# Six DMAs of the first pair begun by GpSimd, and three experts' w2 extended ahead of the first attention pair

## The chip, the cores and the metric

The kernel runs on one core of one Trainium2 chip. The metric is the device time of one execution in microseconds (us), as the median of several. An engine works through its own instructions in the order in which they stand in the program: TensorE (PE in the profile), VectorE (DVE), ScalarE (ACT), GpSimd (POOL), and SyncE (SP), which here only begins DMAs. An engine waits on semaphores for what other engines and DMAs have to deliver, and while it waits, everything behind the waiting instruction on that engine waits too.

## The reference

The kernel computes an attention layer and a mixture-of-experts layer, both with residuals, on an input of 2 x 2048 x 256 floats.

```python
def attention(x):              # 2 x 2048 x 256, one head of width 128
    q, k, v = x @ wq.T, x @ wk.T, x @ wv.T
    q, k = rope(q), rope(k)
    w = softmax(q @ k.T / sqrt(128))
    return (w @ v) @ wo.T

def ffn(z):                    # two loops, 8 experts, the 2 best for each token
    for _ in range(2):
        n = rmsnorm(z, norm_w)
        cw = normalised top-2 of softmax(n @ router_w)
        z = z + sum_e cw[e] * ((silu(n @ w1[e]) * (n @ w3[e])) @ w2[e])
    return z

x = x + layernorm(attention(layernorm(x)))
x = x + layernorm(ffn(layernorm(x)))
```

The expert matrices w1 and w3 are 256 x 512 and w2 is 512 x 256, all in float32. The router's product of the second loop is taken from the expert's output directly: beside w2[e] the kernel keeps w2[e] times the scaled router matrix (512 x 8), so that one matrix product gives a row of the output and its share of the next router logits. Computing these 8 extra columns is what "extending" w2 means.

## The kernel before, in words

The program first projects the input to q, k and v in eight blocks of 512 rows (until about 86 us), then runs attention, then the expert jobs. The change lies in attention.

Attention is written as one loop over `step` (L1593). A query tile has 128 rows; there are 16 for each of the 2 batches, and two tiles make a pair, so pairs 0 to 7 belong to the first batch and 8 to 15 to the second. The scores of a tile are computed in four chunks of 512 keys. Each step works at several stages of the pipeline at once, in this order of the program:

- `move_chunks` (L1465): for the first batch alone, the exponents of a pair are moved by DMA from tile `pr` to a standing area (`wall` in the profile, since it lies in the weights of experts 4 to 7, which are loaded only after pair 7). A chunk takes four DMAs of 128 KB, a pair 16. They begin five steps after the score, at the second tile of a pair.
- `exponents` (L1443): ScalarE, four steps after the score, because the smallest of all four chunks (`nm`) is needed first.
- `turn_chunks` (L1473): VectorE transposes an eighth of the moved pair into `pt`. The first one of a pair (a = 0) needs all 16 moves of that pair.
- `score` (L1424): two matmul instructions, then a reduction on VectorE and after the fourth chunk the one that gives `nm`.
- `values` (L1497), by the table `WHEN` (L1584): the products with v, for pair p at its steps a = 3 to 7 and at a = 0 of the next.
- `leave` (L1510): a generator that is moved on once in every step and brings a finished pair through the output projection and two normalisations; its GpSimd work belongs to it.
- the extension of w2 and the scaling of w1 and w3 (`scale_expert`, L238, GpSimd).

With `p, a = divmod(step - 15, 8)`, pair 0 begins its transposes at step 15, and each pair has the steps a = 0 to 7. Steps 0 to 14 hold the scores of the first tiles and nothing for a pair to turn yet. In pair 6 the scores of six steps are missing, because those of the second batch begin six steps later (`LATER`).

`extend(e)` (L1394) is a generator of six pieces: the load of w2[e] into `wb` (four DMAs of 128 KB begun by SyncE), four transposes on VectorE (`wT`, L1403), and last 16 matmul instructions (`tp_e`, L1411) with a copy by VectorE into place (L1418). In the kernel before, its pieces for expert e stand at the end of the step: the load at a = 5 of pair e - 1, one transpose at each of a = 0 to 3 of pair e, the matmuls and the copy at a = 4. So every pair of the first batch carries one expert, and `wb` has one buffer.

The order on each engine is the order of the program; nothing is rearranged. SyncE begins, in each pair, the moves of the next pair, the load of one w2 and the load of the input rows `xr`.

Of the kernel before, what the change touches and what calls it, by code (L numbers as in the profile page):

```python
# [10 lines left out]
F32 = mybir.dt.float32  # L11
# [8 lines left out]
P = 128  # L20
# [9 lines left out]
def attn_moe_kernel(  # L30
# [16 lines left out]
    nc = tc.nc  # L47

    ctx.enter_context(tc.manual_schedule())
    B, S, D = x.shape  # L50
    HD = wq.shape[0]
    E, _, F = w1.shape
    ND = D // P
    NF = F // P
# [1132 lines left out]
    with tc.tile_pool(name="proj1", bufs=1, **left) as p1, tc.tile_pool(  # L1187
        name="proj", bufs=2, **left
# [190 lines left out]
    with tc.tile_pool(name="prob", bufs=6, **left) as pprob, tc.tile_pool(  # L1379
# [14 lines left out]

        def extend(e):

            wb = pw.tile([P, NF, D], F32, tag="wb", name="wb")
            load_blocks(wb.rearrange("p a d -> p (a d)"), w2[e], 0, NF)
            yield

            wT = pw.tile([P, ND, NF, 4, 32], F32, tag="wT", name="wT")
            for k in range(NF):
                nc.vector.transpose(  # L1403
                    out=wT[:, :, :, k, :].rearrange("p c a t -> p a c t"),
                    in_=wb[:, k, :].rearrange("p (a d c) -> p a c d", a=4, c=ND),
                )
                yield
            ps = ps_t.tile([P, NF, E], F32, tag="tp", name="tp_e")
            for f in range(NF):
                for c in range(ND):  # L1410
                    nc.tensor.matmul(  # L1411
                        ps[:, f, :],
                        lhsT=wT[:, c, f].rearrange("p k t -> p (k t)"),
                        rhs=wr[:, c, :],
                        start=(c == 0),
                        stop=(c == ND - 1),
                    )
            nc.vector.tensor_copy(extended(e) if e < HELD else ext[:, e - HELD], ps)  # L1418
            yield
# [45 lines left out]
        def move_chunks(p, c):  # L1465

            pr = prs.pop((p, c))
            for a in range(4):
                nc.sync.dma_start(
                    out=standing(p)[32 * c : 32 * (c + 1), :, a], in_=pr[32 * a : 32 * (a + 1)]  # L1470
                )

# [116 lines left out]
        first = turns[0][0].before(ps_t, "tp", keep=False)  # L1589
        credit = 0  # L1590
        ahead = iter(range(-GATHER, 0))
        chunks = {u if u // (NT * NKC) in EXCHANGED else u + LATER: u for u in range(NS * NP)}
        for step in range(NS * NP + LEAD + LATER + 1):  # L1593
            u = chunks.get(step - NKC - 1)
            if u is not None and u // (NT * NKC) in EXCHANGED:
                t, c = divmod(u, NKC)
                p, i = divmod(t, QG)
                if i == QG - 1:
                    move_chunks(p, c)
            u = chunks.get(step - NKC)  # L1600
            if u is not None:
                exponents(u)
            p, a = divmod(step - LEAD - LATER, NS)
            if 0 <= p < NP:
                (turn_chunks if p // (NP // B) in EXCHANGED else transposes)(p, a)
            for gen in list(leaving):
                if next(gen, True):
                    leaving.remove(gen)
            if (p, a) >= (ROUTED + 1, 1):
                credit = min(credit, 0) + STEP  # L1610
                while credit > 0:
                    took = next(first, None)
                    if took is None:
                        break
                    credit -= took
                if credit > 0:
                    for m in itertools.islice(ahead, 1):
                        fetch_rows(m)
            u = chunks.get(step)
            if u is not None:  # L1620
                score(u)
            if a == 0 and 0 < p <= NP:
                values(p - 1, NS - 1)
                leaving.append(leave(p - 1))
                next(leaving[-1])
                if p == NP // B:

                    bigs[0].close()
                    rpool = ctx.enter_context(tc.tile_pool(name="route", bufs=1, **right))
                    spool = ctx.enter_context(tc.tile_pool(name="rows", bufs=2, **right))  # L1630
            if 0 <= p < NP:
                for g in WHEN.get(a, ()):
                    values(p, g)
            if a == NS // 2 and HELD <= p - NP // B + HELD < E:
                load_expert(p - NP // B + HELD)
                nc.gpsimd.tensor_copy(
                    extended(p - NP // B + HELD), ext[:, p - NP // B, :, :]
                )
            if a == NS - 3 and -1 <= p < E - 1:
                extending = extend(p + 1)  # L1640
                next(extending)
            elif 0 <= p < E and a < NS - 3:
                next(extending)
            e = p if p < NP // B else p - 1 - NP // B + HELD
            if (0 <= p < HELD or p > NP // B) and e < E:
                if a == 2:
                    scaling = scale_expert(e)
                    next(scaling)
                elif a == 5:
                    next(scaling)  # L1650
# [126 lines left out]
```

## Time and profile before

| | |
|---|---|
| median of 3 runs | 1215.41 us (1214.83 to 1219.23) |
| profiled execution, its own time | 1218.09 us |
| its span (first to last instruction) | 1216.3 us |
| mean granted TensorE clock | 0.985 |
| TensorE busy | 1148.5 us, 94% |
| VectorE, ScalarE, GpSimd busy | 654.4, 426.8, 626.8 us |
| first score | 86.25 us |
| first transpose of pair 0 | 109.03 us |
| first transpose of pair 7 | 235.15 us |
| output of pair 7 leaves PSUM (`oT`) | 257.75 us |

How to read the lines: a line of the timeline has the start in us, the duration, the engine, the line of the program, the operation, the tile written and those read, and the number of instructions; in brackets stands how long the engine was idle before, and what ended the idle time. SPq lines are the times in which SyncE hands over a DMA, not those in which the data moves. In a table of windows the last three columns are the granted TensorE clock (1.00 is full), the mean busy share of the 16 DMA engines, and what they moved in GB/s.

### The profile page before, as it was taken

How to read it: one execution, taken by the hardware profiler on the slowest of the kernel's cores; microseconds unless marked ns; L12 is line 12 of the kernel's file. 1: busy time of each engine (PE TensorE's matmuls, PEld its weight loads, DVE VectorE, ACT ScalarE, POOL GpSimd, SP SyncE). 2: the span in 40 equal slices, each digit the busy share in tenths (PEclk: the TensorE clock that was granted, in tenths of full speed). 3: DMA queues.
4: the chain of work that ended last, by engine and by line, in shares of the span. 5: the costliest groups of instructions: out<-in, count | busy, mean ns of one | idle time of the engine just before them, and what ended most of it. 6: DMA issues, size and time to landing. Idle time of an engine off the chain costs nothing.

```text
span 1216.3 us, 16506 instructions
## 1 busy us (share of the span) xinstructions
PE 1148.5 (94%) x4098; PEld 708.7 (58%) x4098; DVE 654.4 (54%) x1703; ACT 426.8 (35%) x971; POOL 626.8 (52%) x1011
## 2 busy tenths in 40 slices
PE   6987999899989799999999999999999999999995
PEld 4543666566756445555555566556666555565664
DVE  4645888767797377533333558324683333368314
ACT  4444334235544422222222552224522222245224
POOL 3560585455522444455444684455844554478753
PEclk9998999999999999999999999999999999999997
DMA  4715797725301578788877977498664897897825
GB/s 145 212 42 133 167 201 191 166 87 147 105 26 36 145 205 233 197 212 237 230 201 207 278 195 198 147 240 272 218 191 146 233 256 219 227 265 231 257 89 181
DMA packets 229417, 224.15 MB, mean 184 GB/s; under 512 B 83088, under 2 KB 177168, under 8 KB 229328
## 3 DMA queue, kind: packets, MB, share of 16 engines
q1 hardware_dynamic: 205840, 158.98, 48.2%
q0 software_dynamic: 20752, 60.97, 17.5%
q10 hardware_dynamic: 2736, 3.16, 0.8%
q8 instruction: 39, 0.64, 0.2%
q14 instruction: 50, 0.41, 0.1%
HBM read 122.77 MB, written 83.47 MB: 170 GB/s over the span
## 4 chain that ended last, share of the span: by engine, by line
PE 62%; DMA 2%; DVE 1%; issue 1%; ACT 1%; POOL 0%; SPq 0%; ACTq 0%; DVEq 0%; POOLq 0%
PE p L1028 39%; PE py L1087 20%; PE tp_x L1014 1%; PE sum L917 1%; DMA xg<-zd,token 1%; DMA given<-given 0%; DMA zd<-y 0%; PE ps_l L665 0%; DMA xs<-xg 0%; DVE ln_st L198 0%; DMA given<-y,to 0%; SPq L998 0%; DVE z L794 0%; DVE ln_mv L199 0%; ACT z L786 0%
## 5 line engine op out<-in xcount | busy, mean ns | idle before, releaser
L1028 PE MATMUL p<-wall,xT 128*128 x1136 | 513.0, 595 | 5.9 <-ACT a L1037 4.3
L1028 PEld LDWEIGHTS p<-wall,xT 128*128 128x128 f32 x1136 | 211.9, 191 | 218.2 <-issue 207.0
L1101 POOL DMA_INDIRECT given<-y,to x142 | 144.0, 1014 | 303.8 <-ACT y L1100 209.1
L1087 PE MATMUL py<-wall,gT 128*128 x1136 | 272.0, 383 | 2.6 <-ACT y L1100 2.0
L1087 PEld LDWEIGHTS py<-wall,gT 128*128 128x128 f32 x1136 | 215.4, 190 | 94.2 <-issue 64.1
L1053 DVE TENSOR_TENSOR g<-a,p 128x512 f32<-128x512 f32 x138 | 94.5, 684 | 263.2 <-issue 214.3
L1100 ACT ACTIVATE y<-py,rms 128x264 f32<-128x264 f32 (+1 forms) x142 | 67.8, 477 | 315.3 <-PE py L1087 290.0
L969 POOL DMA_INDIRECT xg<-zd,token x142 | 142.0, 1000 | 29.8 <-issue 24.8
L1037 ACT ACTIVATE a<-p,rms 128x512 f32<-128x512 f32 x142 | 97.6, 687 | 151.0 <-PE p L1028 89.4
L1430 PE MATMUL sc<-qkT 128*128 128x512 f32 x256 | 134.9, 621 | 12.0 <-ACT pr L1450 11.2
L1502 PE MATMUL po<-pt,v 128*128 128x256 f32 x512 | 129.3, 386 | 3.5 <-DVE pt L1476 3.1
L1502 PEld LDWEIGHTS po<-pt,v 128*128 128x128 f32 x512 | 98.3, 194 | 56.8 <-issue 35.9
L263 DVE STREAM_TRANSPOSE gT<-gb 128x512 f32<-128x512 f32 x138 | 97.4, 706 | 53.0 <-DMA gb<-gd 46.6
L1450 ACT ACTIVATE pr<-sc,nm 128x512 f32<-128x512 f32 x128 | 87.9, 692 | 97.3 <-DVE nm L1440 64.1
L1437 DVE TENSOR_REDUCE m<-sc 128x1 f32<-128x512 f32 x128 | 87.8, 687 | 36.4 <-PE sc L1430 36.1
L185 POOL TENSOR_TENSOR rds<-rs_v,neg_half 128x2 f32<-128x2 f32 (+1 forms) x24 | 19.8, 823 | 94.3 <-DVE rs_v L184 93.7
L1430 PEld LDWEIGHTS sc<-qkT 128*128 128x128 f32 x256 | 45.0, 196 | 31.0 <-ACT pr L1450 22.0
L1476 DVE STREAM_TRANSPOSE pt<-wall 128x512 f32<-128x512 f32 x64 | 43.8, 686 | 11.4 <-DMA wall<-pr 10.8
L243 POOL TENSOR_SCALAR wall<-wall,nwp 128x1024 f32<-128x1024 f32 x16 | 45.9, 2867 | 0.2
L1273 PE MATMUL pm<-wqkvT,hT 128*128 128x392 f32 x128 | 45.8, 501 | 0.0
L263 DVE STREAM_TRANSPOSE xT<-xb 128x256 f32<-128x256 f32 x88 | 35.8, 408 | 17.6 <-DMA xb<-xs 16.6
L1489 PE MATMUL tp_p<-ident,pr 128*128 128x128 f32 x256 | 40.2, 276 | 5.0 <-ACT pr L1450 3.6
(274 smaller groups left out, 1147.8 us busy)
## 6 DMA issues: line engine op xcount, KB each, us to landing
gd<-g SPq DMA_DIRECT2D x138, 256.0 KB
gb<-gd SPq DMA_DIRECT2D x276, 128.0 KB
wall<-pr SPq DMA_DIRECT2D x128, 128.0 KB
xs<-xg SPq DMA_DIRECT2D x44, 257.0 KB
xb<-xs SPq DMA_DIRECT2D x176, 64.0 KB
given<-given SPq DMA_DIRECT2D x16, 528.0 KB
wall<-in_L_ffn_w SPq DMA_DIRECT2D x16, 512.0 KB
z<-zd POOLq DMA_DIRECT2D x32, 256.0 KB
```

Of the source, the lines that this page charges most:

```text
L263: nc.vector.transpose(out=dst.rearrange("p c (a t) -> p a c t", t=32), in_=src.rearrange(f"p (a {columns}) -> p a c d", a=4, c=dst.shape[1]),)
L969: i = nc.gpsimd.indirect_dma_start(out=self.xg[:, k, :], out_offset=None, in_=zd[self.loop][: (SPLIT if self.i < WHOLE else T) * P, :], in ...
L1028: nc.tensor.matmul(ps, lhsT=self.xT[:, c, :], rhs=wall[:, bass.ds(self.e, 1), o : o + F].rearrange("p o f -> p (o f)"), start=(c == 0), st ...
L1037: nc.scalar.activation(self.a, p1, AF.Silu, scale=self.rms)
L1053: nc.vector.tensor_tensor(g, self.a, self.p3, ALU.mult)
L1087: nc.tensor.matmul(py[:, :w], lhsT=self.gT[:, f, :], rhs=wall[:, bass.ds(self.e, 1), o : o + w].rearrange("p o d -> p (o d)"), start=(f == 0),
L1100: nc.scalar.mul(y, self.py, self.rms)
L1101: i = nc.gpsimd.indirect_dma_start(out=given[self.loop], out_offset=bass.IndirectOffsetOnAxis(ap=self.row(self.turn.to), axis=0), in_=y, i ...
L1430: nc.tensor.matmul(sc[u], lhsT=qkT[b][:, 0, qi * P : (qi + 1) * P], rhs=qkT[b][:, 1, c * KC : (c + 1) * KC], start=True, stop=True,)
L1437: nc.vector.tensor_reduce(nms[t][:, c : c + 1], sc[u], AX.X, ALU.min)
L1450: nc.scalar.activation(prs[p, c][:, i], sc.pop(u), AF.Exp, bias=nms[t], scale=-1.0, accum_out=s4s[t][:, c : c + 1],)
L1502: nc.tensor.matmul(pos[p], lhsT=vn[p * QG // NT][:, 2 * g + j, :HD], rhs=pt[:, j, :], start=(g == 0 and j == 0), stop=(g == NS - 1 and j = ...
```

## The change

Three edits. The tile `wb` gets two buffers. Of the 16 moves of pair 0, six are begun by GpSimd: two of chunks 0 and 2, one of chunks 1 and 3. And the pieces of the extension stand elsewhere: the loads for experts 0 and 1 are issued ahead of the loop; the transposes and matmuls of experts 0, 1 and 2 stand at steps 3 to 7, 8 to 12 and 13 to 17 (the last three of these are a = 0 to 2 of pair 0), with the load for expert 2 after the matmuls of expert 0 at step 7; expert 3 + p stands in pair p for p = 0 to 4, with its load at a = 0, its transposes at a = 3 to 6 and its matmuls at a = 7. Pairs 5, 6 and 7 have none.

```diff
         def extend(e):
-            wb = pw.tile([P, NF, D], F32, tag="wb", name="wb")
+            wb = pw.tile([P, NF, D], F32, tag="wb", name="wb", bufs=2)
             load_blocks(wb.rearrange("p a d -> p (a d)"), w2[e], 0, NF)
             yield
...
             pr = prs.pop((p, c))
             for a in range(4):
-                nc.sync.dma_start(
+
+                engine = nc.gpsimd if p == 0 and a >= 2 + c % 2 else nc.sync
+                engine.dma_start(
                     out=standing(p)[32 * c : 32 * (c + 1), :, a], in_=pr[32 * a : 32 * (a + 1)]
                 )
...
         ahead = iter(range(-GATHER, 0))
+        extendings = [extend(e) for e in range(E)]
+        NFIRST = 3
+        FIRST = {3 + (NF + 1) * e + k: e for e in range(NFIRST) for k in range(NF + 1)}
+        for e in range(2):
+            next(extendings[e])
...
-            if a == NS - 3 and -1 <= p < E - 1:
-                extending = extend(p + 1)
-                next(extending)
-            elif 0 <= p < E and a < NS - 3:
-                next(extending)
+
+            if step in FIRST:
+                next(extendings[FIRST[step]])
+                if step == 3 + NF:
+                    next(extendings[2])
+            if 0 <= p < E - NFIRST and (a == 0 or a > 2):
+                next(extendings[NFIRST + p])
```

## The prediction

> **What bounds the kernel now.** The chain that ended last starts in the expert jobs and says only that TensorE sets the pace there, so I read the attention of the first batch (86 to 258 us) in the timeline, engine by engine. From 260 to 340 us TensorE is busy 19.7 to 20 of every 20 us, and each later stage starts from what the one before delivers, so I count what is won by 258 us as won at the end.
>
> First, SyncE and VectorE around the start of pair 0:
>
> ```profile
> 96.51 10.55 SPq L1469 DMA_DIRECT2D wall<-pr  x16
> 107.10 2.23 SPq L252 DMA_DIRECT2D wb<-in_L_ffn_w  x4
> 109.03 0.71 DVE L1476 STREAM_TRANSPOSE pt<-wall 128x512 f32<-128x512 f32 x1 [5.18 <-DMA wall<-pr]
> 111.37 3.61 PE L1430 MATMUL sc<-qkT 128*128 128x512 f32 x4 [5.67 <-ACT pr L1450]
> ```
>
> SyncE hands over 16 moves at 0.66 us each; the last lands 2.0 us after it was handed over (107.06 to 109.03). VectorE idles 5.18 us for it, TensorE 5.67 us, and afterwards TensorE runs at half clock. The windows of one us tell how full the DMA engines are:
>
> ```profile
> 105.00:106.00 1.00, 0.70 (x2) 0.00 (x0) 0.00 (x0) 0.00 (x0) 0.00 (x0) 1.00 0.90 209
> 109.00:110.00 1.00, 0.00 (x0) 0.00 (x0) 0.97 (x2) 0.00 (x0) 0.00 (x0) 0.50 0.96 208
> 150.00:151.00 1.00, 1.00 (x6) 0.68 (x5) 1.00 (x3) 0.61 (x2) 1.00 (x1) 1.00 0.97 296
> ```
>
> Moves alone run at about 200 GB/s and a share near 0.87; with a store of GpSimd's beside them (`zd<-y`, handed over at 147.98) 296 GB/s. So SyncE's pace and the DMA engines are both near their limit.
>
> Next the later pairs. Pair 3, 5 and 7, each with SyncE's last moves, its w2 load and VectorE's wait:
>
> ```profile
> 160.55 2.25 SPq L252 DMA_DIRECT2D wb<-in_L_ffn_w  x4
> 163.65 0.71 DVE L1476 STREAM_TRANSPOSE pt<-wall 128x512 f32<-128x512 f32 x1 [0.98 <-DMA wall<-pr]
> ...
> 205.22 7.73 SPq L1469 DMA_DIRECT2D wall<-pr  x12
> 213.06 2.82 SPq L252 DMA_DIRECT2D wb<-in_L_ffn_w  x4
> ...
> 224.22 8.12 SPq L1469 DMA_DIRECT2D wall<-pr  x12
> 232.43 2.18 SPq L252 DMA_DIRECT2D wb<-in_L_ffn_w  x4
> 235.15 0.71 DVE L1476 STREAM_TRANSPOSE pt<-wall 128x512 f32<-128x512 f32 x1 [3.56 <-DMA wall<-pr]
> 238.17 0.44 DVE L1403 STREAM_TRANSPOSE wT<-wb 128x256 f32<-128x256 f32 x1 [1.41 <-DMA wb<-in_L_ffn_w]
> 242.35 2.08 PE L1430 MATMUL sc<-qkT 128*128 128x512 f32 x2 [1.97 <-ACT pr L1450]
> 247.63 1.93 PE L1411 MATMUL tp_e<-wr,wT 128*128 128x8 f32 x16
> ```
>
> A loop runs from pair to pair: `nm`, exponents, 16 moves, landing, first transpose, next `nm`. It takes 17.5 to 18 us in pairs 2 to 4 (`nm` at 146.88, 164.98, 182.96, 200.51). TensorE needs nearly as long: 8 scores at 0.86, 8 values at 0.86, 1.1 for the output projection, 1.7 for `tp_e` (its start to the next start), 16.6 us in all. Twice more the clock falls to half, after a `tp_e` and after idle stretches:
>
> ```profile
> 211.00:212.00 1.00, 1.00 (x2) 0.34 (x1) 0.34 (x1) 1.00 (x5) 1.00 (x1) 0.50 0.89 213
> 245.00:246.00 1.00, 1.00 (x4) 0.74 (x3) 0.80 (x2) 0.00 (x0) 1.00 (x2) 0.50 0.00 0
> ```
>
> **The change part by part** (a minus is time won).
>
> *Loads ahead of the loop (experts 0, 1).* 8 DMAs on SyncE, which has nothing to hand over between 60 and 96 us, at a DMA share of 0.15: nothing, unless the buffers come free only when the projection ends at 86 us; then they land by 92 us, still in time for steps 3 and 8.
>
> *Expert 0 in steps 3 to 7.* Four transposes of 0.43 us between the reductions. I followed VectorE: before, `nm` of the second tile stood at 95.47; two of the transposes fall into its gap of 1.49 us at 91.5, the others delay it to about 95.9. So the exponents that the moves need come 0.4 us later.
>
> *Expert 2's load at step 7* waits on SyncE for expert 0's last transpose (95 us), takes 2.2 us, and the moves stand behind it: they begin at 97.5 instead of 96.5.
>
> *Six moves on GpSimd.* It is idle from 93.2 to 131.1 once its scaling (8.5 us) is done, and that now comes after the moves, with 20 us to spare. Handing over 256 KB costs it 0.66 to 0.83 (`x1d<-xr`). SyncE's ten take 6.6 us: last one at 104.1, first transpose at 106.1 if handing over is the limit. If the DMA engines are: moves need 0.87 x 10.5 = 9.1 us of them and w2 2.7 (rest of the shares to 111 us), from 97 us on, so 109.8 at worst. And VectorE, with expert 1's copy waiting for `tp_e` at step 12, comes to this transpose at 106.8. I take 107.8, between the ends: -1.2 (-2.9 to +0.8). The Trainium skill, "DMA: Bandwidth & Descriptors", section "Issuing engines are not separate DMA queues", speaks against this edit: DMAs begun by several engines share the same 16 DMA engines, and a second issuer saves only handing-over time, usually little. By that rule this term is +0.8; by the row of 296 GB/s there is room.
>
> *Pair 0* now holds `tp_e` of experts 2 and 3: +1.7 on TensorE, which ran without a gap from 111.37 to 128 us. Against it, TensorE idles less ahead of it (I get 2.8 instead of 5.67 us, since `tp_e` of expert 1 and the later scores fill it), which may save the half clock that cost 1.5 us: +0.9 (+0.2 to +1.7).
>
> *Pairs 1 to 4.* One expert each as before, and SyncE's slots are the same: the load at a = 0 is handed over straight after the same moves as the one at a = 5 was. Gone are VectorE's waits for `wb` (0.7, 0, 1.0, 0.4 us), but they come after `nm` and beside the loop. New is that the copy waits for `tp_e` at a = 7, just ahead of the next pair's first transpose, the reduction and `nm`, instead of after `nm` at a = 4 (0.7 to 1.5 us). In pairs 2 to 4 the moves land later than that: 0 (-1.5 to +2.0).
>
> *From pair 5's moves on no w2 stands in the queue.* Before, the last move landed 2.8 to 4.2 us after hand-over where w2 followed, 2.0 without load. Pair 5's start: -0.8 (-1 to 0). Pair 5: from 18.5 us (`nm` 200.51 to 219.02, with `tp_e` and 1.8 lost to half clock) to the loop's 16: 1.0 to the first move, 11.4 for moves and `xr`, 2.0 landing, 1.4 to `nm`; TensorE needs 14.9 plus gaps: -2.5 (-3 to -1). Pair 6 is set by moves alone (219.02 to 235.15), so its extension was hidden: -0.8 by landing (-1 to 0).
>
> *Pair 7.* VectorE's `nm` comes 1.4 (wait) + 0.7 (two transposes) earlier, so the scores at 242.35 do too: -2.1; `tp_e` on TensorE: -1.7; half clock from 241 to 247.5 cost 2.7 us, of which I take half: -1.2. Together -5.0 (-6.5 to -3.5).
>
> Sum: -1.2 + 0.9 + 0 - 0.8 - 2.5 - 0.8 - 5.0 = -9.4. The profiled execution (1216.3 span, 1218.09 in all) would go to 1208.7; it stands 2.7 above the median, and from the median I get 1206.0.
>
> **The rivals.**
>
> *A, slower: half clock in every early pair.* At 210 us the clock fell right after a `tp_e` with only 0.48 us of idle before it. Now `tp_e` stands next to the wait for `oT` (0.46 us in every pair), in pairs 0 to 4. A fall costs 1.8 us (as in pair 5) to 3.2 us (as from 241 us); five of them 9 to 16. Above 1.9 us each all is lost, at 3.2 the time is 1222. Against it: pairs 1 to 4 have the same matmuls and gaps of 0.34 and 0.46, and their rows show 1.00. The skill's "TensorE: Matmul & The Clock Gate", "Why this matters for your kernels", warns only of idle gaps above about 3 us; by that A costs nothing, but the row at 210 us has the fall without such a gap.
>
> *B, pair 0 starts late.* If GpSimd's moves land late, or w2 of expert 2 holds up the others, the first transpose goes to 111 or 112 us: +2 to +3 in place of -1.2, which leaves 1209 to 1211.
>
> *C, the moves set the pace anyway.* If pair 5 gains only its landing (-1), pair 7 only `tp_e` and the wait (-3), the sum is -4 and the time 1211.
>
> **How the numbers follow.** The forecast 0.58 (its own range 1200.5 to 1210.5, terms added with part of their bounds), C 0.20, B 0.10, A 0.12. All bounds together reach from 1200 to 1215; leaving A's tail and the last of the low end out gives 1200 to 1214. About 0.5% (6 us) can be told from no change. Faster: 0.54 of the forecast, 0.07 of C, 0.03 of B: 0.64. Slower: most of A, 0.09. The rest 0.27.
>
> **What would show it.** First transpose of pair 0 at 106 to 108.5 us, with VectorE's wait under 2 us; pairs 1 to 4 still 17.5 to 18.5 us; `nm` to `nm` in pair 5 near 16; no `tp_e` after pair 4; `oT` of pair 7 near 248 instead of 257.75; the clock at 1.00 in pair 5. Wrong, if pairs 1 to 4 grow by a us each, or if pair 7 still waits several us after its first transpose.

## The result, and the profile after

The changed kernel took 1221.07 us (median of 14 runs, 1216.56 to 1223.84) against 1215.56 us for the kernel before on the same chip: a ratio of 1.0038 [1.0025, 1.0050]. That is slower by some 4.6 us, inside the half per cent that was to count as no change, and far from the 1206 forecast. The profiled execution has a span of 1219.4 us and a mean granted clock of 0.980 (before: 1216.3 us and 0.985).

The landmarks tell where it went. "T" is the first transpose of pair 0; a pair runs from its first transpose to that of the next, pair 7 to the start of its `oT`. Both kernels were profiled a second time (the runs `x13` and `x14` below), and both executions are given.

| us | before | after | mean change | forecast |
|---|---|---|---|---|
| T | 109.03, 108.98 | 112.09, 110.67 | +2.4 | -1.2 |
| pair 0 | 17.00, 17.33 | 22.17, 21.82 | +4.8 | +0.9 |
| pairs 1 to 4, to pair 5's start | 73.16, 72.84 | 74.36, 75.72 | +2.0 | -0.8 |
| pair 5 | 18.13, 17.86 | 18.00, 16.94 | -0.5 | -2.5 |
| pair 6 | 17.83, 17.84 | 16.42, 16.31 | -1.5 | -0.8 |
| pair 7, to `oT` | 22.60, 21.33 | 16.79, 17.11 | -5.0 | -5.0 |
| `oT` of pair 7 at | 257.75, 256.18 | 259.83, 258.57 | +2.2 | -9.4 |

What the sum of 2.2 us lacks to 4.6 I can't place: behind `oT` of pair 7 the span goes on for 958 to 965 us in the twenty profiles of this study, and that spread hides it.

First the start of pair 0, in the timeline of SyncE, GpSimd and VectorE of the changed kernel:

```profile
85.62 12.90 SPq L252 DMA_DIRECT2D wb<-in_L_ffn_w  x12
98.63 8.06 SPq L1471 DMA_DIRECT2D wall<-pr  x10
106.80 2.48 SPq L252 DMA_DIRECT2D wb<-in_L_ffn_w  x4
...
98.89 3.48 POOL L1471 DMA_DIRECT2D wall<-pr  x6 [14.22 <-ACT pr L1450]
...
112.09 0.71 DVE L1478 STREAM_TRANSPOSE pt<-wall 128x512 f32<-128x512 f32 x1 [2.02 <-DMA wall<-pr]
```

The moves were handed over as planned, but the first transpose comes 5.4 us after SyncE's last hand-over (106.69 to 112.09), not 2.0 us as before. The load of expert 2 stands directly ahead of the moves (96.6 to 98.5 us), since it waits for expert 0's last transpose. The loads of experts 0 and 1 are handed over at 85.6 to 89.7 us, when the projection's buffers come free, and they are through before the moves begin: the DMA share is 0.00 at 94 to 96 us.

Then TensorE behind its wait, and the clock:

```profile
114.44 2.08 PE L1430 MATMUL sc<-qkT 128*128 128x512 f32 x2 [3.79 <-ACT pr L1450]
116.31 3.42 PE L1411 MATMUL tp_e<-wr,wT 128*128 128x8 f32 x16
119.58 2.05 PE L1430 MATMUL sc<-qkT 128*128 128x512 f32 x2
121.43 2.99 PE L1504 MATMUL po<-pt,v 128*128 128x256 f32 x8
```

```profile
112.00:116.00 4.00, 1.56 (x2) 0.79 (x3) 3.87 (x8) 2.39 (x7) 0.00 (x0) 0.68 0.39 57
116.00:120.00 4.00, 4.00 (x18) 3.69 (x17) 0.96 (x4) 0.39 (x2) 0.00 (x0) 0.50 0.88 203
120.00:124.00 4.00, 4.00 (x9) 2.49 (x9) 2.24 (x4) 0.00 (x0) 0.00 (x0) 0.54 0.87 199
```

(The third number from the end of a window is the granted clock.) The same windows of the kernel before:

```profile
112.00:116.00 4.00, 4.00 (x10) 2.06 (x9) 3.67 (x8) 1.33 (x4) 0.00 (x0) 0.66 0.74 172
116.00:120.00 4.00, 4.00 (x23) 3.24 (x21) 2.65 (x6) 1.17 (x3) 0.00 (x0) 1.00 0.70 158
```

Before, the clock was back at 1.00 at 114.7 us, 3.3 us after TensorE's wait had ended (111.37); here it stays at half until 123.7 us, 9.3 us after the wait (114.44), and `tp_e` of the third expert takes 3.42 us instead of the 1.85 it takes at full clock. The moves of pair 1 do not set the length of pair 0 here: their last hand-over ends at 124.8 us, 9.5 us ahead of the first transpose of pair 1 (134.3); before, it was 2.2 us.

The steps of pairs 1 to 4 have turned round, too. VectorE at the start of pair 4:

```profile
190.58 0.19 DVE L1418 COPY ext<-tp_e 128x32 f32<-128x32 f32 x1 [1.11 <-PE tp_e L1411]
190.95 0.71 DVE L1478 STREAM_TRANSPOSE pt<-wall 128x512 f32<-128x512 f32 x1 [0.18 <-issue]
192.27 0.16 DVE L1440 TENSOR_REDUCE nm<-m 128x1 f32<-128x4 f32 x1
```

The first transpose of the pair no longer waits for the moves. It waits for the copy of `tp_e`, and `nm`, which lets the next exponents begin, comes behind both. The end is as forecast: no w2 stands in pair 7, and its span is 5.0 us shorter. SyncE, VectorE and ScalarE of the changed kernel:

```profile
232.19 8.16 SPq L1471 DMA_DIRECT2D wall<-pr  x12
243.04 0.71 DVE L1478 STREAM_TRANSPOSE pt<-wall 128x512 f32<-128x512 f32 x1 [3.66 <-DMA wall<-pr]
247.06 0.16 DVE L1440 TENSOR_REDUCE nm<-m 128x1 f32<-128x4 f32 x1
259.83 0.37 ACT L1522 COPY oT<-po 128x256 f32<-128x256 f32 x1 [1.75 <-PE po L1504]
```

`nm` comes 4.0 us after the pair's first transpose (243.04 to 247.06) instead of 6.2 (235.15 to 241.33), and no `tp_e` follows.

### The profile page after: what moved, and what is told of

Its sections match the earlier page's. It is cut to its first block, busy times and chain, and to the rows that moved or that the text cites. A ratio compares the mean times of both kernels' runs of the same rounds, so it can differ in the third digit from the quotient of the medians.

```text
span 1219.4 us, 16525 instructions
## 1 busy us (share of the span) xinstructions
PE 1155.1 (95%) x4098; PEld 712.6 (58%) x4098; DVE 656.6 (54%) x1703; ACT 425.3 (35%) x971; POOL 630.5 (52%) x1017
## 4 chain that ended last, share of the span: by engine, by line
PE 56%; DMA 5%; SPq 2%; issue 2%; DVE 1%; ACT 1%; POOL 0%; ACTq 0%; DVEq 0%; POOLq 0%
PE p L1028 36%; PE py L1087 18%; DMA gd<-g 1%; DMA given<-given 1%; PE tp_x L1014 1%; DMA gb<-gd 1%; DMA xg<-zd,token 1%; SPq L998 1%; PE sum L917 1%; SPq L1065 1%; DMA zd<-y 0%; PE ps_l L665 0%; DVE ln_st L198 0%; DMA given<-y,to 0%; ACT y L1100 0%
## 5 line engine op out<-in xcount | busy, mean ns | idle before, releaser
L1430 PE MATMUL sc<-qkT 128*128 128x512 f32 x256 | 137.6, 633 | 5.6 <-ACT pr L1450 4.8
L185 POOL TENSOR_TENSOR rds<-rs_v,neg_half 128x2 f32<-128x2 f32 (+1 forms) x24 | 19.8, 824 | 89.6 <-DVE rs_v L184 89.0
L1430 PEld LDWEIGHTS sc<-qkT 128*128 128x128 f32 x256 | 47.5, 203 | 22.9 <-issue 10.5
L263 DVE STREAM_TRANSPOSE xT<-xb 128x256 f32<-128x256 f32 x88 | 35.7, 407 | 17.6 <-DMA xb<-xs 15.8
```

The source lines that it names most:

```text
L263: nc.vector.transpose(out=dst.rearrange("p c (a t) -> p a c t", t=32), in_=src.rearrange(f"p (a {columns}) -> p a c d", a=4, c=dst.shape[1]),)
L1430: nc.tensor.matmul(sc[u], lhsT=qkT[b][:, 0, qi * P : (qi + 1) * P], rhs=qkT[b][:, 1, c * KC : (c + 1) * KC], start=True, stop=True,)
```

## The experiments

All ratios are against the kernel before on the same chip, with the 95% interval. T and the pairs are as above, from the profile of each run; "pair 1 to `oT`" is the time from the first transpose of pair 1 to `oT` of pair 7, and the column after it is when that `oT` starts. "Old steps" means that the experts not extended ahead of the pairs have their pieces where the kernel before has them; "early" means that w2 of the experts extended ahead is loaded at about 60 us.

| run | edit to the changed kernel, in short | T | pair 0 | pair 1 to `oT` | `oT` at | ratio |
|---|---|---|---|---|---|---|
| before | | 109.0 | 17.0 | 131.7 | 257.8 | 1 |
| after | | 112.1 | 22.2 | 125.6 | 259.8 | 1.0038 [1.0025, 1.0050] |
| x1 | all moves by SyncE | 113.8 | 22.6 | 125.6 | 262.0 | 1.0040 [1.0016, 1.0063] |
| x2 | before, with the six moves on GpSimd | 109.3 | 17.2 | 131.7 | 258.2 | 0.9990 [0.9967, 1.0012] |
| x3 | two experts ahead, old steps | 113.1 | 17.3 | 125.9 | 256.3 | 0.9963 [0.9947, 0.9979] |
| x6 | two experts ahead | 110.2 | 18.6 | 127.7 | 256.5 | 0.9970 [0.9944, 0.9997] |
| x4 | w2 of the three loaded early | 109.8 | 22.3 | 125.8 | 257.8 | 1.0004 [0.9988, 1.0020] |
| x5 | x4 with the old steps | 112.8 | 22.8 | 122.5 | 258.1 | 0.9966 [0.9949, 0.9984] |
| x7 | two ahead, early, old steps, SyncE | 113.4 | 17.2 | 125.1 | 255.7 | 0.9924 [0.9899, 0.9948] |
| x8 | one ahead, early, old steps, SyncE | 111.1 | 17.5 | 123.6 | 252.2 | 0.9942 [0.9922, 0.9962] |
| x12 | x8, its load at 86 us | 109.2 | 17.1 | 124.5 | 250.8 | 0.9945 [0.9931, 0.9958] |
| x9 | x5, third expert's matmuls at a = 6 | 109.9 | 20.2 | 123.2 | 253.3 | 0.9934 [0.9918, 0.9950] |
| x10 | x5, TensorE kept busy before pair 0 | 112.5 | 20.4 | 123.0 | 255.9 | 0.9945 [0.9928, 0.9962] |
| x11 | x8, TensorE kept busy before pair 0 | 111.6 | 15.6 | 124.6 | 251.8 | 0.9930 [0.9917, 0.9943] |
| x17 | x8, no w2 load behind the first moves | 111.0 | 17.4 | 125.3 | 253.7 | 0.9956 [0.9930, 0.9981] |
| x18 | x17 with the six moves on GpSimd | 109.2 | 17.0 | 124.2 | 250.3 | 0.9954 [0.9927, 0.9980] |
| x15 | waits ahead of the first scores filled | 110.2 | 22.4 | 125.4 | 257.9 | 1.0026 [1.0009, 1.0042] |
| x16 | x7, both stretches filled | 110.1 | 15.7 | 124.5 | 250.3 | 0.9948 [0.9930, 0.9965] |

**Who begins the moves.** `x1` takes GpSimd's part back out of the changed kernel, `x2` puts that part alone into the kernel before.

```diff
-                engine = nc.gpsimd if p == 0 and a >= 2 + c % 2 else nc.sync
+                engine = nc.sync
```

> The changed kernel with all 16 moves of pair 0 begun by SyncE again. Theory D (the DMA engines are the limit of the start: between 98 and 113 us they run at a share of 1.0 to 1.3 and some 210 GB/s, so who begins a move does not matter): first transpose of pair 0 again at 111 to 113 us (112.09 in the changed kernel), time within 2 us of the changed kernel's 1221. Theory I (handing over is the limit, and GpSimd's part saved 4 us): first transpose at 115 to 116, time 1224 to 1226.

> The kernel before with nothing but the six moves of pair 0 begun by GpSimd. Theory D: first transpose of pair 0 at 108 to 109.5 us (109.03 before), time within 1.5 us of before. Theory I: first transpose at 105.5 to 106.5, time 2 to 4 us below before.

Neither moved the time. T of `x1`, 113.8 us, lies between what the two theories gave; 1.3 of the 1.75 us by which it is later than in the changed kernel were lost before the moves, since `nm` of the second tile came at 98.50 instead of 97.20 us. In `x2` the hand-over on SyncE ends at 104.9 instead of 107.1 us, and the first transpose comes at the same time:

```profile
96.56 8.34 SPq L1470 DMA_DIRECT2D wall<-pr  x10
104.94 2.23 SPq L252 DMA_DIRECT2D wb<-in_L_ffn_w  x4
...
109.34 0.71 DVE L1477 STREAM_TRANSPOSE pt<-wall 128x512 f32<-128x512 f32 x1 [5.45 <-DMA wb<-in_L_ffn_w]
```

The w2 that SyncE now hands over sooner mixes with the moves, and at 100 to 104 us the DMA engines move 238 GB/s instead of 198. So it could be that two queues do move more, and that the w2 took the gain. `x17` and `x18` take this w2 away: one expert is extended ahead, w2 of the first two is loaded early, and no load stands behind the first moves. `x18` has six of the moves on GpSimd, `x17` none.

```diff
-            if a == NS - 3 and -1 <= p < E - NFIRST - 1:
+            if a == NS - 3 and 0 <= p < E - NFIRST - 1:
                 next(extendings[NFIRST + p + 1])
...
-            if e < NFIRST:
+            if e < 2:
                 o = 2 * QG * S + e * NF * D
...
-        for e in range(NFIRST):
+        for e in range(2):
             next(extendings[e])
```

(the diff is to `x8`, below).

> One expert ahead, w2 of the first two experts loaded at about 60 us and the others by the old steps, all moves by SyncE: no load of w2 stands behind the first pair's moves any more, for either theory. With one expert ahead and a load behind the moves T (first transpose of pair 0) was 109.2 us at full clock, 2.0 us after the last hand-over at 107.1. Theory D (the DMA engines set the start): without the w2 behind them the moves land no later than before, T 108.5 to 109.3 us (later by 1.6 to 3 if the first scores fall to half clock). Theory I (handing over sets it): T 109.0 to 109.3, the same. Ratio 0.992 to 0.996.

> The same with six of the first pair's moves begun by GpSimd, as in the change. With a load of w2 behind the moves GpSimd's part was worth nothing (0.9990), but the moves and that load together ran at 238 GB/s at 100 to 104 us instead of 198, and SyncE handed the load over 2.2 us sooner. Theory D, strict form (moves begun by two engines run at the 200 GB/s of one): T as in the run with SyncE alone, within 0.3 us, counted from the second tile's nm. Theory Q (two queues do move more, and what they won went to the w2 that came sooner): 238 GB/s or more at 100 to 104 us, T 1 to 2 us earlier than with SyncE alone, counted from the second tile's nm: 107 to 108 us at full clock; ratio lower by 0.1%, which three rounds can't tell.

From `nm` of the second tile to T it took 13.4 us with SyncE alone (97.53 to 110.96) and 13.7 us with GpSimd (95.48 to 109.18), so there is no gain even then, and the ratios are the same. Windows of `x18`, and one of `x17` below them:

```profile
100.00:104.00 4.00, 3.07 (x7) 1.03 (x5) 2.51 (x5) 0.94 (x3) 3.97 (x4) 0.86 1.05 229
104.00:106.00 2.00, 2.00 (x5) 0.95 (x6) 0.78 (x2) 1.85 (x6) 2.00 (x1) 1.00 1.04 202
106.00:108.00 2.00, 1.60 (x4) 0.38 (x2) 0.61 (x1) 0.00 (x0) 2.00 (x2) 1.00 0.83 153
108.00:109.00 1.00, 0.00 (x0) 0.00 (x0) 0.00 (x0) 0.00 (x0) 1.00 (x1) 1.00 0.00 0
...
110.00:111.00 1.00, 0.00 (x0) 0.00 (x0) 0.04 (x1) 0.00 (x0) 0.00 (x0) 0.80 0.35 74
```

The 229 GB/s of the first four us are not held: once GpSimd's moves are through (at 104.8 us), what is left runs at about 200. The last data of the moves is through at 107.8 us in `x18`, 11.3 us after the first hand-over, and at 110.6 in `x17`, 12.0 us after it. So two engines did bring the data 0.7 us sooner. But T comes 1.4 us after the last data in `x18` and 0.4 us after it in `x17`, and nothing is gained: from the first hand-over to T it takes 12.5, 12.4 and 12.7 us in `before`, `x17` and `x18`. By the trace the last move is reported complete at 108.7 us in `x18`, 0.9 us after its data, and at 110.9 in `x17`, 0.3 us after it, and VectorE, idle by then, starts 0.5 and 0.1 us later. Why the report comes so late behind moves of two engines is not shown. The w2 behind the moves is not what the start waits for. The page of the Trainium skill that the prediction weighed ("DMA: Bandwidth & Descriptors", "Issuing engines are not separate DMA queues") says that a second issuer saves only handing-over time, and the runs are on its side.

**Two experts instead of three.** `x3` extends two ahead and puts the others back to the steps of the kernel before; `x6` extends two ahead and keeps the new steps.

```diff
-        NFIRST = 3
+        NFIRST = 2
...
-                if step == 3 + NF:
-                    next(extendings[2])
-            if 0 <= p < E - NFIRST and (a == 0 or a > 2):
+            if a == NS - 3 and -1 <= p < E - NFIRST - 1:
+                next(extendings[NFIRST + p + 1])
+            elif 0 <= p < E - NFIRST and a < NS - 3:
                 next(extendings[NFIRST + p])
```

> The changed kernel with two experts ahead of the pairs instead of three, and the others at the steps of the kernel before (load at a = 5 of the pair ahead, transposes at a = 0 to 3, matmuls at a = 4), in pairs 0 to 5. Theory S (a third expert's matmuls in pair 0 at half clock, and the matmuls at a = 7 where they wait for a late transpose, cost pairs 0 to 4 about 6 us): nm to nm of pair 0 17.5 to 19 us instead of 22.2, pair 3 18 instead of 19.7, oT of pair 7 at 252 to 255, time 1213 to 1216. Theory D alone (only the loads ahead of the first moves cost): pair 0 still 21 to 22 us, time 1219 to 1221.

> Two experts ahead, with loads and steps as in the changed kernel (transposes at a = 3 to 6, matmuls at a = 7, now in pairs 0 to 5). Theory P: first transpose of pair 0 to that of pair 1 at 17 to 19 us, time near the run with two ahead and the old steps (0.996 to 0.998 of before). Theory S: this pair above 20 and one of pairs 1 to 4 at 19.5 or more, time 1.000 to 1.004 of before.

Both are faster than the kernel before, by the same within their intervals. Pair 0 is back at 17.3 and 18.6 us, so the third expert makes pair 0 long. (`oT` of `x3` is later than expected, since T is 113.1 us.) Pair 3 takes 17.6 us in `x3` and 19.8 in `x6`, so the new steps do cost time there, as theory S has it. Between old and new steps the two ratios do not decide, though pair 1 to `oT` is 1.8 us shorter with the old ones.

**The loads early, and the old steps with three experts.** The third part of the standing area is not written before the moves of pair 2. `x4` loads w2 of the three experts there at about 60 us. `x5` adds the old steps for the other five, for which `wT` needs a second buffer.

```diff
-            wb = pw.tile([P, NF, D], F32, tag="wb", name="wb", bufs=2)
+            if e < NFIRST:
+                o = 2 * QG * S + e * NF * D
+                wb = stand[:, o : o + NF * D].rearrange("p (a d) -> p a d", a=NF)
+            else:
+                wb = pw.tile([P, NF, D], F32, tag="wb", name="wb")
...
-        for e in range(2):
+        for e in range(NFIRST):
             next(extendings[e])
...
-                if step == 3 + NF:
-                    next(extendings[2])
```

> The changed kernel with w2 of the three experts loaded at 60 us into a part of the standing area that no pair uses before pair 2, so that none of these loads waits for the projection's buffers or runs between 86 and 100 us. Theory D: first transpose of pair 0 at 107 to 109.5 us instead of 112.09, time 1217 to 1219. Theory M (what delays the start are the extension's matmuls and transposes between the scores, and half clock): first transpose still at 111 or later, time 1220 to 1222.

> Three experts ahead with their loads at 60 us, wT with two buffers, and the other five at the steps of the kernel before. Theory P (the third expert's matmuls in pair 0, met by a half clock, make this pair 5 us longer): first transpose of pair 0 to that of pair 1 still 20 to 23 us, time within 2 us of the kernel with early loads alone (1.000 of before). Theory S (it is the late steps a = 3 to 7): this pair at 17 to 18.5, pair 3 under 18.5, time 5 to 7 us below it (0.994 to 0.996).

Early loads bring the ratio from 1.0038 to 1.0004, which is more than the profiles show: T of `x4` is 0.9 us earlier than in the second profile of the changed kernel, and `oT` 0.7 us. The old steps with the second `wT` buffer bring it on to 0.9966. Of the two theories for `x5`, P was right about pair 0 (22.8 us) and S about pair 3, which takes 19.8 us in `x4` and 18.0 in `x5`. TensorE in pair 3 of `x4`, and the clock:

```profile
166.52 1.95 PE L1415 MATMUL tp_e<-wr,wT 128*128 128x8 f32 x16 [0.98 <-DVE wT L1407]
171.57 1.25 PE L1551 MATMUL py_t<-woT,oT 128*128 128x264 f32 x2 [0.46 <-ACT oT L1526]
...
169.00:170.00 1.00, 1.00 (x4) 0.63 (x3) 1.00 (x2) 0.00 (x0) 1.00 (x1) 0.67 1.00 191
170.00:171.00 1.00, 1.00 (x3) 0.33 (x1) 0.93 (x6) 0.00 (x0) 0.70 (x3) 0.50 0.23 39
```

and TensorE of `x5`:

```profile
163.98 1.85 PE L1415 MATMUL tp_e<-wr,wT 128*128 128x8 f32 x16
174.20 0.71 PE L1551 MATMUL py_t<-woT,oT 128*128 128x264 f32 x2 [0.46 <-ACT oT L1526]
```

With the new steps `tp_e` waits 0.98 us for VectorE's last transpose of w2 and stands just ahead of the next `nm`. The clock falls to half at 169.3 us, behind `tp_e` and ahead of the wait for `oT` (in the changed kernel it stands at half from 171.4 to 174.9 us). All six profiles with the new steps show this fall in pair 3 and a length of 19.8 us; none of the fourteen with the old steps does (17.2 to 18.2 us). With the old steps `tp_e` waits for nothing there, and the copy comes after `nm`. `x3`, `x7` and `x8` have the old steps and a single `wT` buffer and take 17.6 to 18.2 us, so the steps do it, not the buffer.

**How many ahead are worth it.** `x7` and `x8` have two and one, with early loads, old steps, all moves by SyncE and one `wT` buffer. `x12` is `x8` with its load at 86 us, by the second `wb` buffer of the change.

```diff
-        NFIRST = 3
+        NFIRST = 2
```

> Two experts ahead with their loads at 60 us, the others at the old steps, all moves by SyncE. Theory D (the loads at 86 us cost the start, by half clock at the first scores or by the share of the DMA engines): first nm at 90.5 to 91, first transpose of pair 0 at 108.5 to 110, oT of pair 7 at 251.5 to 254, time 0.993 to 0.995 of before. Rival (the loads are not the reason for the late first scores): first nm at 92 to 94 again, time 0.996 as with the loads at 86 us.

```diff
-        NFIRST = 3
+        NFIRST = 1
```

> The same with one expert ahead, the others in pairs 0 to 6. Theory L (what is won is won in pair 7 alone, since the extension of the pairs before it lies beside moves that set their pace): pair 7 from its first transpose to oT at 17 to 18.5 us instead of 22.6, time as with two ahead, within 0.001. Theory E (each pair freed counts alike): half of what two ahead win, 0.9965 to 0.9975 of before.

```diff
-        for e in range(2):
+        for e in range(1):
             next(extendings[e])
```

> The kernel with one expert early as before, but its w2 loaded at 86 us, when the projection's buffers come free, as in the change, instead of at about 60 us. If w2's loads at 86 us cost time of their own (they take DMA engines and queue ahead of the first pair's moves): ratio 0.996 to 0.998 against 0.9942, first transpose of pair 0 0.5 to 2 us later than the 111.1 us there. If only three loads one behind the other do, and one of 0.8 MB or less lands before the first moves: the same 0.993 to 0.996, first transpose within 0.5 us but for what the clock at the first scores does (half clock there costs 1.6 to 3 us with or without such loads).

`x7` met neither forecast: its first scores ran at half clock with no load beside them (first `nm` at 93.6 us, T at 113.4), as the rival said, and yet its ratio is the lowest of all. So the half clock at the first scores needs no load at 86 us. One expert ahead gets what two get, as far as the intervals tell (0.9924 and 0.9942 differ by more than the 0.001 forecast, but overlap), and `x12` shows that one load of 0.5 MB at 86 us costs nothing (T at 109.2 us). Pair 7 takes 16.8 us in `x8` and in `x12`, against 22.6 and 21.3 before: it is the emptied pair 7 that is won. Clearing pair 5 was worth little. Its length goes with the clock: where a fall lies in it, it takes 17.7 to 18.1 us with an expert at the old steps (seven profiles) and 17.3 to 18.0 without (four); at full clock 16.9 and 17.1 with one (`x8`, `x16`; but 18.4 and 18.3 in `x3` and `x17`, behind a fall in pair 4) and 16.6 to 17.4 without (four).

**Is it the third expert's work or the clock?** `x9` moves its matmuls from step 17 to step 21 (a = 6 of pair 0). `x10` leaves them and adds four matmuls as large as a score, whose result nobody reads, in TensorE's wait.

```diff
+        FIRST[21] = FIRST.pop(17)
```

> The kernel with three experts extended between the first scores, their w2 loaded early and the old steps for the others (pair 0 took 22.8 us there, ratio 0.9966), with the third expert's 16 matmuls of 8 columns moved from step a = 2 of pair 0 to step a = 6, where the clock is full in all other kernels. Theory H (they hold pair 0 up because they stand where TensorE has just come out of its wait at half clock, and a further wait of 0.91 us for the turned w2 starts that anew): pair 0 takes 18 to 19 us, full clock from about 119 on, ratio 0.993 to 0.995. Theory W (it is the third expert's work itself, about 3 us of matmuls and the turns on VectorE, wherever it stands in the pair): pair 0 stays at 21 to 23 us and the ratio at 0.996 to 0.998.

```diff
+            if step == 16:
+                warm = ps_t.tile([P, KC], F32, tag="tp", name="warm")
+                for _ in range(4):
+                    nc.tensor.matmul(warm, lhsT=qkT[0][:, 0, :P], rhs=qkT[0][:, 1, :KC],
+                                     start=True, stop=True)
```

> The same kernel with three experts early and the old steps, its third expert's matmuls left at a = 2 of pair 0, and four matmuls of the size of a score added (work added, their result unused) in the 4.56 us in which TensorE waits for the first pair's moves at 110.6 to 115.1 us. Theory H (the half clock after the wait is what makes pair 0 slow): granted clock 1.00 from 108 to at least 117, pair 0 18 to 20 us instead of 22.8, ratio 0.993 to 0.995. Theory W (the third expert's work itself): clock full, yet pair 0 at 21 us or more, ratio 0.996 to 0.998.

Both take pair 0 from 22.8 to a little over 20 us, between what the two theories gave, and both ratios are 0.2 to 0.3% below that of `x5`, with intervals that touch or overlap. So it is some of each: in `x9` half of the excess of 5.3 us over the 17.5 of `x8` goes with the place of the matmuls, and the other half stays with the work. In `x9` the clock is full from about 118 us, although `tp_e` still runs later in the pair (windows of `x9`):

```profile
112.00:116.00 4.00, 3.75 (x5) 1.69 (x6) 3.48 (x8) 2.21 (x8) 0.00 (x0) 0.50 0.48 113
116.00:120.00 4.00, 4.00 (x13) 2.93 (x12) 2.64 (x6) 0.00 (x0) 0.00 (x0) 0.71 0.86 199
120.00:124.00 4.00, 4.00 (x26) 3.37 (x25) 1.44 (x4) 2.79 (x8) 0.00 (x0) 1.00 0.88 203
```

`x10` tells why its gain was not larger. TensorE:

```profile
110.11 3.60 PE L1636 MATMUL warm<-qkT 128*128 128x512 f32 x8
114.86 1.12 PE L1434 MATMUL sc<-qkT 128*128 128x512 f32 x2 [1.15 <-ACT pr L1454]
117.27 2.21 PE L1415 MATMUL tp_e<-wr,wT 128*128 128x8 f32 x16 [1.29 <-DVE wT L1407]
119.34 2.05 PE L1434 MATMUL sc<-qkT 128*128 128x512 f32 x2
```

The clock stayed full over the wait, and then fell just before 119 us, behind two waits of only 1.15 and 1.29 us, the second of them the third expert's own wait for its turned w2.

**Without the third expert.** `x11` puts six such matmuls into the wait of `x8`:

```diff
+            if step == 16:
+                warm = ps_t.tile([P, KC], F32, tag="tp", name="warm")
+                for _ in range(6):
...
```

> The kernel with one expert early (its w2 loaded at about 60 us, old steps, all moves by SyncE; ratio 0.9942, pair 0 17.5 us with half clock at 112 to 117), with six score-sized matmuls added (work added, their result unused) in TensorE's wait of 5.73 us before pair 0. Theory H: clock 1.00 from 96 to 128, pair 0 15.5 to 16.5 us, 1 to 2 us less: ratio 0.992 to 0.994. Rival (pair 0 is set by the moves and VectorE's transposes, not by TensorE): clock full, pair 0 still 17 to 17.5 us, ratio 0.994 to 0.995; if the added matmuls run into the scores that follow, slower, 0.995 to 0.997.

The clock is 1.00 from 112 to 120 us (`x8`: 0.50 and 0.78 in the two windows), and pair 0 takes 15.6 instead of 17.5 us. Windows of `x11`:

```profile
112.00:116.00 4.00, 4.00 (x11) 1.73 (x10) 2.29 (x6) 2.78 (x8) 0.00 (x0) 1.00 0.66 114
116.00:120.00 4.00, 4.00 (x18) 3.16 (x17) 4.00 (x9) 0.00 (x0) 0.00 (x0) 1.00 0.79 184
```

So pair 0 hangs on TensorE's clock. In the whole time it hardly shows: `oT` of pair 7 is 0.4 us earlier, because the clock fell at other places (100 to 103 us, which the expectation had not seen, and 212 to 216), and the ratios of `x8` and `x11` overlap.

**The half clock at the first scores.** In the first profile of the changed kernel the first scores ran at half clock, and T was 1.4 us later than in the second one. The same kernels were profiled again without any edit, and `x15` fills the three short waits ahead of the first scores with seventeen small transposes of the identity (work added).

```diff
                 for t in range(G):
                     nc.tensor.transpose(tp[:, t, :], qk[:, t, j, :], ident)
+                    for _ in range({1: 5, 2: 7}.get(t, 0) if n == NB - 1 and j == 0 else 0):
+                        nc.tensor.transpose(tp[:, 3, :], ident, ident)
...
+            if n == NB - 1:
+                pm = ps_m.tile([P, 3 * HD + E], F32, tag="pm", name="pm")
+                for _ in range(5):
+                    nc.tensor.transpose(pm[:, :P], ident, ident)
```

> The changed kernel once more, nothing altered, for its clock at the first scores. Two theories of the half clock at 86 to 90 us, which eight of the fourteen profiles so far show. T (toss): TensorE's three short waits ahead of the first scores (0.74, 1.03 and 0.74 us in every kernel) lie at the edge of what the clock bears, and it falls or not from execution to execution, whatever the kernel: the profile may show 1.00 at 86 to 90 and the first reduced minimum at 90.7 us. C (cause in the change): half clock again, first minimum at 92 to 94 us.

> The kernel before once more, nothing altered. Theory T: half clock at 86 to 90 us is as likely as not, with the first minimum then at 92 to 94 us. Theory C: full clock and 90.7 us again.

> The changed kernel with seventeen small TensorE transposes of the identity added (work added, their result unused) in the three waits ahead of the first scores, at 82.6, 83.7 and 85.5 us. Theory T, and theory C too if the waits are how the clock falls: clock 1.00 from 80 to 94, first minimum at 90.6 to 91.0 us, first transpose of pair 0 at 109.5 to 110.5 us instead of 112.1, pair 0 still 22 us, ratio 1.001 to 1.003. If the clock falls for another reason than the waits: half clock at 86 to 90 all the same, ratio 1.0038 as before.

The same window of the changed kernel, first profile:

```profile
86.00:90.00 4.00, 3.77 (x5) 1.70 (x6) 0.82 (x2) 0.18 (x1) 0.00 (x0) 0.57 0.94 167
```

and second profile:

```profile
86.00:90.00 4.00, 3.89 (x9) 1.82 (x10) 2.22 (x4) 0.06 (x1) 0.00 (x0) 1.00 0.93 171
```

In the same program the clock fell in one execution and not in the other, with the same waits ahead (0.73, 1.03 and 0.74 us). Of the eighteen profiles with those waits, nine show the fall; the two with the waits filled (`x15`, `x16`) do not, but two executions are too few to prove that the filling does it. The kernel before was seen twice, both times at full clock, so whether it falls as well stays open. With or without the fall the changed kernel is late: T is 110.7 us in the second profile and 110.2 in `x15`, pair 0 still takes 22 us, and the ratio of `x15` is 1.0026.

**Both stretches filled with two experts ahead.** `x16` is `x7` with `x15`'s filling and five of `x10`'s matmuls:

```diff
+            if step == 16:
+                warm = ps_t.tile([P, KC], F32, tag="tp", name="warm")
+                for _ in range(5):
...
```

> The kernel with two experts early (w2 loaded at about 60 us, old steps, all moves by SyncE; ratio 0.9924), with the same small transposes ahead of the first scores and five score-sized matmuls in TensorE's wait before pair 0 (work added, their result unused). If the clock in both waits is what is left: clock 1.00 from 80 to 128, first minimum 90.7 instead of 93.6 us, first transpose of pair 0 at 110 to 111 us instead of 113.4, pair 0 15.5 to 16.5 us instead of 17.2, 2 to 4 us less in all: ratio 0.989 to 0.991. If time won early is lost again at the later waits: 0.9915 to 0.993.

The clock is 1.00 up to 228 us, T is 110.1 us, and `oT` of pair 7 comes at 250.3 us, as early as in any run. Yet the ratio is 0.9948, outside both forecasts and no better than `x7`. The 5.5 us between the two at `oT` are those of one execution each, and `x7`'s was its slowest of six (1217.53 us against its median of 1211.65), so they say little of the other runs. Time won at the start by a full clock was not seen again in the whole time in `x11` or in `x16`. The best versions are `x7`, `x11`, `x9`, `x8`, `x10`, `x12` and `x16`, 0.5 to 0.8% faster than the kernel before, and their intervals overlap.

## Why the prediction was wrong

Its mechanism for the end was right: pair 7 without an expert is 5.0 us shorter, as the sum had it, and `nm` comes 2.2 us earlier in the pair (1.8 in the second executions) where 2.1 was forecast. The start was wrong by 7.5 us (T and pair 0), and further steps missed.

- *Six moves on GpSimd, T at 107.8.* The step took a row of 296 GB/s, of moves beside a store, as room for moves beside moves. For T there was none: `x2` moved it by +0.3 us, and `x18` against `x17` shows the same with no load behind. The DMA end of the bounds ("109.8 at worst") was the nearer one, though its parts, 97 + 9.1 + 2.7, make 108.8; even 109.8 is passed: T is 110.7 us at full clock. Early loads do not bring it back to 109.0 (109.8 in `x4`), one expert ahead does (109.2 in `x12`). Why the second and third expert's work delays T without a load is not shown.
- *The loads ahead of the loop, "nothing".* The text named the condition, that the buffers come free only at 86 us, and it held, with the two loads through before 94 us, nearly as it said; one load there cost nothing (`x12`). What collides with the moves is expert 2's load at step 7. Early loads for all three (`x4`) gained 0.34% on the changed kernel.
- *Pair 0, +0.9.* This is the largest miss: +4.8, and the step that failed most. It counted `tp_e` of the third expert at its full-clock price (+1.7) and hoped for a half clock saved (-0.8). But `tp_e` stands right behind TensorE's wait, and with it there the half clock lasts over 9.3 us of TensorE's work instead of 3.3. Half of the difference, 3.0 us, is an estimate of what the clock took; with 1.7 for the work it makes 4.7. `x9` and `x10` get about 2.5 us back each by moving the matmuls or by keeping TensorE busy; without the third expert pair 0 is 15.6 to 18.6 us in every run.
- *Pairs 1 to 4, 0 (-1.5 to +2.0), and pair 5's start, -0.8.* Measured +2.0 together. The text saw that the copy now stands ahead of the first transpose and `nm`, and set it at nothing since the moves landed later. They no longer do: the transpose waits for the copy. Pair 1 is 1.1 us shorter all the same and pair 2 only 0.4 longer; the cost lies in pair 3, 1.8 and 2.2 us longer in the two executions, where the clock falls behind a `tp_e` that waits. In the second execution pair 4 has such a fall too, and is 1.5 us longer.
- *Landing, -0.8 at pair 5's start and in pair 6.* The text took 2.0 us from the last hand-over to the first transpose for the time without a load behind. But that is pair 0, where a load of w2 was handed over straight behind (107.10), as its own rows show. In pairs 6 and 7 of the changed kernel, with no load left, it is 2.6 to 2.9 us, against 2.8 and 3.1 in pair 7 before. Pair 6 gained 1.5 us all the same, but only some 0.3 of it by landing; the rest lies between its first transpose and the last hand-over. The sign was right by luck.
- *Pair 5, -2.5.* Measured -0.5. It took the loop to be set by the w2 load and `tp_e`; in `x8` the pair takes 16.9 us with both. What made it 18 us is the fall of the clock at 209 to 212 us, which came in the first profile of the changed kernel too, and not in the second (16.9 us).

Of the rivals, B was right about T (111 to 112 us forecast, 112.1 and 110.7 measured), but not alone. C was right about pair 5, and wrong about pair 7. A was right that falls of the clock decide, that they come behind a `tp_e` with a short wait, and that 3 us without work are not needed for them; but not each early pair alike has one: pair 0 holds most of it, pair 3 has one in both executions and pair 4 in one. The page it was weighed against ("TensorE: Matmul & The Clock Gate") warns in its rule of idle gaps above some 3 us; by the rows here the clock fell behind a single wait of 0.98 us, after waits of 1.15 and 1.29 us in a row, and after 0.73, 1.03 and 0.74 in half of the executions. Its section "What's actually happening" says more fitly that a free-running window of activity decides, so that the point of a transition varies from run to run; the two executions of the changed kernel are in keeping with that, but no run here tests it.

## What to carry to other kernels

Work that is moved into the start of a pipeline is priced by the clock and the queue that it finds there: matmuls put right behind a wait run at half clock and, with a short wait of their own, can keep it low. Ask which single piece of the moved work buys the gain; here emptying the last pair bought nearly all of it, one expert ahead of the loop was enough, a second added nothing that the intervals show, and the third brought a load and matmuls to the crowded start and cost time. Before sharing out DMAs over two engines, check whether the data or the handing over arrives last.

## What the runs showed of the hardware

- The granted clock falls to half behind waits well below 3 us, and the same program may or may not fall at such a place (0.57 and 1.00 at 86 to 90 us). Of the `tp_e` groups that began at full clock up to 235 us in the twenty profiles, 71 had a wait ahead of them (0.15 to 1.3 us), and 32 of these were followed by a fall, 1.5 to 3.1 us after their start; of the 79 without a wait none was. What decides between the 32 and the others is not shown.
- In the attention of the first batch each stretch at half clock lasted 3.4 us or a whole multiple of it (6.8 us before pair 0 in the kernel before, 10.2 in the changed one).
- Sixteen matmuls of 8 columns took 1.85 us at full and 3.42 us at half clock. After the wait ahead of pair 0 (3.0 to 5.8 us where it was not filled) and with only larger matmuls behind it the clock was back after 3.2 to 6.1 us; with the small ones among the first it took 8.5 to 10.8.
- Moves within SBUF begun by one engine ran at about 200 GB/s with a busy share near 0.87. Begun by two they reached 229 GB/s and a share of 1.05 for a few us. The data of the 2 MB was through 0.7 us sooner, but the first transpose of it did not start sooner. SyncE's ten hand-overs beside GpSimd's took 8.3 us in `x2`, 0.83 each on average instead of 0.66.
